# Six small moves in a two-layer gated cross-attention kernel: queues, PSUM rings and a halved last store

## The chip, the cores and the metric

The kernel runs on one core of a Trainium2 chip. A core has five engines with their own instruction queues: TensorE (PE, matrix products into PSUM), VectorE (DVE), ScalarE (ACT), GpSimd (POOL) and SyncE (SP, which here only starts transfers). ACT and POOL can start transfers too. Transfers run on 16 DMA engines beside them. The metric is the device time of one execution in microseconds (us).

## The reference

There are 16 sequences of 128 tokens with 512 features, and for each a context of 128 latents with 128 features. Two layers follow one another, each with an attention over the context and a feed-forward part, and each part is added to x through a gate:

```
x = x + tanh(g_xattn[0]) * L0_xattn(layernorm(x), ctx)   # 8 pairs of heads, low rank, rotary keys, softmax
x = x + tanh(g_ffn[0])   * L0_ffn(layernorm(x))          # 512 -> 2048 -> 512, LoRA experts, the best 2 of 8
x = x + tanh(g_xattn[1]) * L1_xattn(layernorm(x), ctx)   # 16 heads of 32, causal softmax
x = x + tanh(g_ffn[1])   * L1_ffn(layernorm(x))          # softmax-weighted sum of 8 products of rank 64
```

In layer 0 the query passes through three weights (Wq, w_kc_q and the rope weights W_qr) that don't depend on the tokens, so they can be multiplied together once. In layer 1 scores are q·k / sqrt(32) with later positions masked, and the feed-forward part is out = sum over k of alpha_k · U_k (V_k x), with alpha = softmax(relu(x W1 + b1) W2 + b2). Everything is float32.

## The kernel before

All matrix products have 128 rows of PSUM and 128 to 512 columns; four sequences (512 tokens) make a group g = 0 to 3. Sequences are loaded in the order 8 to 15, 0 to 7.

*Folding (L522 to L550).* The queries' three weights are folded into one, fq, pair of heads by pair of heads (p = 0 to 7): m_ps multiplies the rope weights wqr by wcq (L522), mT and mtr turn the product, f_ps (L546) multiplies it by wq. SP brings wcq, wqr and wq; ACT's queue brings the first wqr, the cosines and sines, the first four token tiles (256 KB each, L510), wkr and the gates. Between the folds, TensorE computes the keys k_ps0 and queries q_ps0 of the first group. VectorE takes the statistics of the first four token tiles as they land (L145, L146), ACT the root (L148), VectorE normalises (L158).

*Layer 0, attention.* The eight pairs of sequences are walked through with an order written out by hand. At the same time TensorE computes o_ps, the products of the output weight; VectorE and ACT copy them and VectorE and GpSimd form their sums (L632 to L640). `turn(v)` (L457) transposes two normalised token tiles on TensorE; only for v = 2 does it stand between the o_ps. Scores go through maximum (L685), exponential (ACT L696), reciprocal (L701), normalisation on GpSimd (L703), transposition within 32x32 blocks on VectorE (L709) and 16 sends by SP that move the blocks into eT.

*Layer 0, feed-forward.* For each group, `up_pair` computes the products hs_ps and ht_ps of a pair of hidden blocks in a form with fewer products, `spread` computes t_ps, the first low-rank products of all experts, and masks them by the chosen experts (L372), `adapt_pair` adds them (l_ps), and `down` multiplies back to 512 features. For groups 1 to 3 `spread` runs in the tail of the group before; for group 0 it follows the first `up_pair`.

*Layer 1.* A loop s = 2 to 17 has, in each step, `values` and `project` of sequence s − 2 (o_ps, y_ps), `score` of sequence s (v_ps and the scores s_ps, followed by L1316, L189, ACT L194, L199, GpSimd L201 and the transposition L1322 into eb), and `carry(s)`: ten 64 KB sends from eb to eT. Between these, a list `fill` of other units is taken by a table `plan`: queries (q_ps), and for the feed-forward part `hidden` (h_ps), `share_parts`, `ranks` (vx_ps) and `mixture` (my_ps). At s = 2, 6 and 10 `latents` transposes the latents of the next group (kv1tr_1 to kv1tr_3), and kv1tr_0 comes ahead of the loop. `tokens(g)` turns a group's normalised tokens by 16 sends, `ffn_tokens(g)` the same for the feed-forward part (xf).

*What sets the order.* TensorE and SP run in program order where `ordered` is set; VectorE's, ACT's and GpSimd's order is made by a scheduler from the dependences. An engine executes its queue in order, so one waiting instruction holds up all behind it. PSUM has three rings of 128x512 tiles: `ps_mm` with 4, `ps_tr` with 2 and `ps_acc` with 2 buffers; a tile can be written only when the reader of the tile that held its buffer before is done. In layer 1 q_ps, v_ps, h_ps, kv1tr and odd my_ps are in `ps_tr`, o_ps, y_ps and even my_ps in `ps_acc`. `evacuate` (L85, L87) copies PSUM by turns on VectorE and ACT; `drain` (L1204) copies on VectorE while a flag `near` is set and goes through `evacuate` otherwise. Transfers of SP and ACT share eight semaphores in turn, so each waits until the one eight before it has landed; those of GpSimd have eight of their own. `send` (L179) is a transfer on SP; `shared_send` (L1242) puts every third on GpSimd's queue and the others on SP.

Of the kernel before, what the change touches and what calls it, by code (L numbers as in the profile page):

```python
# [11 lines left out]
ALU = mybir.AluOpType  # L12
# [4 lines left out]
NB = 16  # L17
D = 512
ND = D // P
GB = 4  # L20
NG = NB // GB
# [21 lines left out]
def kernel(  # L43
# [9 lines left out]
    nc = tc.nc  # L53
# [9 lines left out]
    def mm_tile(name):  # L63
        return ps_mm.tile([P, 512], F32, tag="mm", name=name)

    def tr_tile(name):
        return ps_tr.tile([P, 512], F32, tag="tr", name=name)
# [7 lines left out]
    def pin(ins):  # L75
        if pinned[0]:
            tc.keep_in_program_order(ins)
# [33 lines left out]
    xs, xt = [None] * NB, [None] * NB  # L111

    def place(n):
        return (n + KEPT) % NB
# [11 lines left out]
    gate_f = [gates[:, 2 + i : 3 + i] for i in range(2)]  # L126
# [41 lines left out]
    def matmul(*args, **kw):  # L168
        ins = nc.tensor.matmul(*args, **kw)  # L169
        if ordered[0]:  # L170
            tc.keep_in_program_order(ins)

    def transpose(*args):
        ins = nc.tensor.transpose(*args)
        if ordered[0]:
            tc.keep_in_program_order(ins)
# [29 lines left out]
    half = GT // 2  # L206
# [154 lines left out]
    def spread(q):  # L361

        g = q.g
        t_ps = tr_tile(f"t_ps{g}")
        for c in range(ND):
            matmul(
                t_ps, a1_sb[:, c, :], q.xnT[:, c, :], start=(c == 0), stop=(c == ND - 1)
            )
        q.t1 = []
        for k in range(2):  # L370
            t = fh.tile([P, GT], F32, tag=f"t1_{k}", name=f"t1_{g}_{k}")
            nc.vector.scalar_tensor_tensor(  # L372
                t, t_ps, LORA_SCALE, q.selT[k], ALU.mult, ALU.mult
            )
            q.t1.append(t)


    with tc.tile_pool(name="a0", bufs=2) as ap, tc.tile_pool(name="a0s", bufs=3) as sp:
# [72 lines left out]
        def turn(v, which=(0, 1)):  # L451
            g, h = divmod(v, 2)
            if h == 0 and which[0] == 0:
                turned[g] = lnp.tile([P, ND, GT], F32, tag="xnT", name=f"xnT_a0_{g}", bufs=1)
            for i in which:
                xn = xns[v][i]
                tr = tr_tile(f"xtr_a0_{v}_{i}")  # L457
                for c in range(ND):
                    transpose(tr[:, ts(c, P)], xn[:, ts(c, P)], ident)
                dst = turned[g][:, :, ts(2 * h + i, P)]  # L460
                if v == 2:
                    pin(nc.vector.tensor_copy(dst, tr.rearrange("p (c t) -> p c t", t=P)))
                else:
                    evacuate(dst, tr.rearrange("p (c t) -> p c t", t=P))
# [5 lines left out]
        for kept, tag in ((k_r, "ca"), (q_r, "cb")):  # L470
            t = ap.tile([P, NPAIR, 2 * P], F32, tag=tag, name=f"{tag}_kq", bufs=1)
# [3 lines left out]
        with tc.tile_pool(name="fold", bufs=3, side="right") as fp:  # L475
# [31 lines left out]
            nc.scalar.dma_start(out=cos_sb, in_=cos_t)  # L507
            nc.scalar.dma_start(out=sin_sb, in_=sin_t)
            for n in range(GB):
                nc.scalar.dma_start(out=xs[n], in_=x[place(n)])  # L510
            nc.scalar.dma_start(out=wkr_sb, in_=wkr)
            nc.scalar.dma_start(out=gates[:, 0:2], in_=g_x.partition_broadcast(P))
            nc.scalar.dma_start(out=gates[:, 2:4], in_=g_f.partition_broadcast(P))
# [47 lines left out]
            for p in range(NPAIR):  # L561
# [13 lines left out]
                else:  # L575
                    tr = tr_tile("kvtr_0")
# [324 lines left out]
        for u in range(1, last + 1):  # L901
# [3 lines left out]
            v = u - 1  # L905
# [108 lines left out]
    for n in range(KEPT):  # L1014
        b = place(n)
# [48 lines left out]
    def up_pair(q, m):  # L1064

        g = q.g
        w = ups.pop((g, m))
        far = m + NF // 2
        bias, bias_f = bias1_sb[:, m : m + 1], bias1_sb[:, far : far + 1]


        ps = [tr_tile(f"hs_ps{g}_{m}_{n}") for n in range(2)]
        ps += [mm_tile(f"ht_ps{g}_{m}_{n}") for n in range(2)]

        def product(bank, cols, n):
            dst = ps[bank][:, cols]
            for c in range(2):
                matmul(dst, w[:, n, c, :], q.rhs[n][:, c, :], start=c == 0, stop=c == 1)
            return dst

        def part(name):
            return fh.tile([P, half], F32, tag=name, name=f"{name}_{g}_{m}", bufs=2)

        def biased_sum(dst, product, bias, other):
            nc.vector.scalar_tensor_tensor(dst, product, bias, other, ALU.add, ALU.add)

        base = tp.tile([P, GT], F32, tag="t", name=f"base_{g}_{m}")
        base_f = tp.tile([P, GT], F32, tag="t", name=f"base_{g}_{far}")
        p1, u2, u3, u4 = part("p1"), part("u2"), part("u3"), part("u4")
        nc.scalar.copy(p1, product(0, lo, 0))  # L1090
        biased_sum(base[:, lo], product(1, lo, 1), bias, p1)
        nc.vector.tensor_tensor(u2, product(2, lo, 4), p1, ALU.add)
        nc.vector.tensor_tensor(u3, product(0, hi, 5), u2, ALU.add)
        p5 = product(1, hi, 3)
        nc.vector.tensor_tensor(u4, p5, u2, ALU.add)
        biased_sum(base_f[:, hi], p5, bias_f, u3)
        biased_sum(base[:, hi], product(2, hi, 6), bias, u4)
        biased_sum(base_f[:, lo], product(3, lo, 2), bias_f, u3)
        if m + 2 < NF // 2:
            load_up(g, m + 2)  # L1100
        elif g + 1 < NG:
            load_up(g + 1, m + 2 - NF // 2)
        return base, base_f
# [98 lines left out]
    def drain(dst, src):  # L1202
        if near[0]:
            nc.vector.tensor_copy(dst, src)  # L1204
        else:
            evacuate(dst, src)
# [7 lines left out]
    kv, kvT, xa, ks, qs = {}, {}, {}, {}, {}  # L1214
# [3 lines left out]
        send(kv[g], kvc[g * GB : (g + 1) * GB].rearrange("b l d -> l b d"))  # L1218

    def latents(g):  # L1220
        tr = tr_tile(f"kv1tr_{g}")
        for i in range(GB):
            transpose(tr[:, ts(i, P)], kv[g][:, i, :], ident)
        kvT[g] = le.tile([P, GT], F32, tag="kvT", name=f"kv1T_{g}")
        drain(kvT[g], tr)
        if g + 1 < NG:
            load_latents(g + 1)

# [17 lines left out]
    def turn_all(dst, src, share=False):  # L1246

        for n, (t, k) in enumerate((t, k) for t in range(NK) for k in range(NK)):
            ends = dst[ts(k, BK), :, ts(t, BK)], src[ts(t, BK), :, ts(k, BK)]
            shared_send(n if share else 0, *ends)  # L1250
# [21 lines left out]
    def tokens(g, xb):  # L1272

        if g == 2:
            xa[g] = ap.tile([P, ND, GT], F32, tag="xf", name="xnT_a1_2", bufs=1)
        else:
            xa[g] = lnp.tile([P, ND, GT], F32, tag="xnT", name=f"xnT_a1_{g}", bufs=1)
        turn_all(xa[g].rearrange("p c (i t) -> p (c i) t", i=GB), xb)

    def queries(g, c):  # L1280
        q_ps = tr_tile(f"q1_ps{g}_{c}")
# [78 lines left out]
    xf, hs, al, avT, lTs = {}, {}, {}, {}, {}  # L1360
# [96 lines left out]
    def mixture(b):  # L1457
# [7 lines left out]
        residual(b, y_ps, gate_f[1])  # L1465
        done.append(b)

    done = []

    def store(keep):  # L1470
        while len(done) > keep:
            b = done.pop(0)
            send(out[b], xt[b])
# [34 lines left out]
    q = first  # L1508
    for g in range(NG):
        last = g == NG - 1  # L1510
        held = None
        for m in range(NF // 2):
            bases = up_pair(q, m)
            if g == 0 and m == 0:
                spread(q)
            if held is not None:
                adapt(q, m - 1, held)
            held = adapt_pair(q, m, bases)
            if g > 0 and m == 3:
                for b in range((g - 1) * GB, g * GB):  # L1520
                    moments1(b)
        if last:
            deviations1(slice(0, g * GB))
            aqo_sb = wp.tile([P, 2 * ND, D], F32, tag="w16", name="aqo_sb")
            for n, w in enumerate((a_wqT, a_woT)):
                send(aqo_sb[:, n * ND : (n + 1) * ND, :], w.rearrange("(c p) d -> p c d", p=P))
            xb = fh.tile([P, H, P], F32, tag="T", name="xb_a1_0")
            standard(xb, 0, mv1, rstd1, "a1", q.mixed)
            tokens(0, xb)
        else:  # L1530
            nxt = measure(g + 1)
            blocks(nxt, fh.tile([P, ND, GB, P], F32, tag="T", name=f"xb_f0_{g + 1}"),
                   q.mixed)
            turn_blocks(nxt)
        down(q, 0)
        adapt(q, NF // 2 - 1, held)
        bias_out(q)
        second_ranks(q)
        if last:
            break  # L1540
        for n in range(1, 7):
            down(q, n, {
                2: lambda: route_parts(nxt), 6: lambda: spread(nxt),
            }.get(n))
            if n == 2:
                route(nxt)
                quarter_tokens(nxt)
            elif n == 3:
                send_chosen(nxt)
        q = nxt  # L1550
# [11 lines left out]
    xb = le.tile([P, H, P], F32, tag="eT", name="xb_a1_1", bufs=1)  # L1562
# [23 lines left out]
    mw_sb = ap.tile([P, 3 * ND, D], F32, name="mw_sb", bufs=1)  # L1586
# [5 lines left out]
    for s in range(AHEAD, NB + AHEAD):  # L1592
        b = s - AHEAD
# [37 lines left out]
        if s in (3, 5, 7):  # L1631
            n = s // 2 - 1
# [6 lines left out]
    g = NG - 1  # L1639
# [8 lines left out]
    store(1)  # L1648
    for unit in units(ranks, g):
        unit()  # L1650
    for b in range(g * GB - 1, NB):
        mixture(b)
        store(1)
    store(0)

# [68 lines left out]
```

## Time and profile before

| quantity | value |
|---|---|
| time of three runs | 1509.08, 1509.17 (median), 1509.71 us |
| the profiled execution | 1511.77 us, span 1510.0 us, mean granted clock 0.998 |
| busy: TensorE | 1481.4 us, 98% of the span |
| busy: VectorE, ScalarE, GpSimd | 838.7 (56%), 436.6 (29%), 474.7 us (31%) |
| moved | 163.50 MB |

The profile is of one execution; the span runs from its first to its last instruction. "Waits" lists for each kind of instruction of an engine what ended the idle time before it: total, number, longest. "Timeline" lists instructions in order of time with start and duration, equal neighbours drawn together; in brackets is the idle time of the engine ahead of it and what ended it. The table by stage gives, for each stretch, its length, the busy time of the five engine columns (TensorE, its weight loads, VectorE, ScalarE, GpSimd) with counts, the granted TensorE clock, the DMA engines' busy share and GB/s. For a transfer the trace also has the moment at which it landed. A number behind a tile's name (o9, xn_0, eT(10)) says which sequence, group or pair it belongs to.

### The profile page before, as it was taken

To read this page: it belongs to the slowest core of one execution; us is meant where nothing else is said; L and a number is where in the kernel's file an instruction comes from. 1 tells how busy PE (TensorE), PEld (TensorE's weight loads), DVE (VectorE), ACT (ScalarE), POOL (GpSimd) and SP (SyncE) were. 2 spreads that over 40 slices of the span, in tenths; PEclk is the share of its full clock that TensorE was granted. 3 is DMA by queue.
4 is the path that set the end of the run, shared out by engine and by line. 5 is a ranking of instruction groups with operands and counts; after the bars stand their busy time and mean duration, and the time that the engine had idled before them with its cause. 6 is when DMAs were issued, how large, how long until landed. Compare 5 with 4: busy or idle time off the path is not lost. (4 is left out here: it accounts for less than half of the span.)

```text
span 1510.0 us, 19474 instructions
## 1 busy us (share of the span) xinstructions
PE 1481.4 (98%) x6744; PEld 996.9 (66%) x6744; DVE 838.7 (56%) x1723; ACT 436.6 (29%) x1430; POOL 474.7 (31%) x495
## 2 busy tenths in 40 slices
PE   8999999999999999999999999999999989999998
PEld 5667778878877666876678667866667444444444
DVE  3275654554566555655574656465756766747422
ACT  2252433443331222012211221022123555445310
POOL 2052633632522244113420433133313333424200
PEclk9999999999999999999999999999999999999999
DMA  9335567444446611642245224522253463535312
GB/s 318 105 77 92 146 178 178 96 113 100 91 77 161 232 63 70 157 138 73 74 112 158 74 74 105 144 94 73 74 137 72 69 113 71 89 54 85 69 28 98
DMA packets 360130, 163.50 MB, mean 108 GB/s; under 512 B 286528, under 2 KB 334400, under 8 KB 357856
## 3 DMA queue, kind: packets, MB, share of 16 engines
q1 hardware_dynamic: 356608, 156.54, 41.8%
q0 software_dynamic: 1856, 3.80, 1.8%
q10 hardware_dynamic: 1568, 1.90, 0.4%
q8 instruction: 54, 0.88, 0.3%
q14 instruction: 44, 0.36, 0.1%
HBM read 106.35 MB, written 18.09 MB: 82 GB/s over the span
## 5 line engine op out<-in xcount | busy, mean ns | idle before, releaser
L1124 POOL TENSOR_TENSOR near<-base,a 128x512 f32<-128x512 f32 x32 | 41.9, 1311 | 347.2 <-ACT base L1121 193.2
L703 POOL TENSOR_TENSOR e<-e,rden_a 128x512 f32<-128x512 f32 x64 | 66.1, 1040 | 181.8 <-DVE rden_a L701 181.8
L169 PE MATMUL l_ps<-t,b_sb 128*128 128x512 f32 x256 | 115.2, 592 | 1.4 <-DVE t L372 1.4
L169 PE MATMUL q_ps<-xnT_a,fq 128*128 128x256 f32 (+1 forms) x448 | 115.8, 410 | 0.0
L1121 ACT ACTIVATE a<-a 128x512 f32<-128x512 f32 x64 | 40.3, 629 | 257.3 <-DVE a L1120 257.3
L696 ACT ACTIVATE e<-s_ps,nmx_a 128x128 f32<-128x128 f32 x256 | 90.2, 384 | 80.9 <-DVE nmx_a L685 41.1
L201 POOL TENSOR_TENSOR e<-e,rden_a 128x512 f32<-128x512 f32 x64 | 66.4, 1039 | 149.6 <-DVE rden_a L199 147.4
L194 ACT ACTIVATE e<-e,nmx_a 128x128 f32<-128x128 f32 x256 | 98.8, 387 | 37.3 <-DVE nmx_a L189 37.3
L1120 DVE TENSOR_TENSOR a<-l_ps,base 128x512 f32<-128x512 f32 x64 | 44.0, 688 | 108.3 <-PE l_ps L169 108.3
L169 PEld LDWEIGHTS q_ps<-xnT_a,fq 128*128 128x128 f32 x448 | 84.8, 190 | 24.5 <-issue 12.5
L1186 DVE SCALAR_TENSOR_TENSOR x<-fy_ps,gw,x 128x256 f32<-128x256 f32 x112 | 46.5, 476 | 78.3 <-PE fy_ps L169 78.3
L169 PEld LDWEIGHTS l_ps<-t,b_sb 128*128 128x128 f32 x256 | 48.6, 190 | 61.7 <-issue 57.6
L169 PE MATMUL fy_ps<-ring,far 128*128 128x256 f32 x384 | 87.2, 380 | 0.0
L169 PE MATMUL y_ps<-fo_raw,c 128*128 128x256 f32 x384 | 85.8, 380 | 0.9 <-DVE c L85 0.9
L770 DVE SCALAR_TENSOR_TENSOR x<-y_ps,gates,x 128x256 f32<-128x256 f32 x112 | 48.7, 477 | 65.9 <-PE y_ps L169 65.8
L169 PEld LDWEIGHTS fy_ps<-ring,far 128*128 128x128 f32 x384 | 72.6, 190 | 13.6 <-issue 4.0
L169 PEld LDWEIGHTS y_ps<-fo_raw,c 128*128 128x128 f32 x384 | 72.3, 190 | 10.7 <-ACT c L87 1.0
L169 PE MATMUL ht_ps<-T,ring 128*128 128x256 f32 x256 | 65.7, 379 | 0.0
L169 PE MATMUL t_ps<-a,a_sb 128*128 128x512 f32 x128 | 65.4, 592 | 0.0
L169 PE MATMUL t_ps<-base,a_sb 128*128 128x512 f32 x128 | 65.4, 592 | 0.0
L169 PE MATMUL q_ps<-xnT_a,aqo_sb 128*128 128x512 f32 x128 | 59.8, 614 | 2.6 <-DMA xnT_a<-late 1.9
L169 PE MATMUL y_ps<-fo_sums,c 128*128 128x256 f32 x256 | 60.8, 385 | 1.5 <-DVE c L85 0.8
(256 smaller groups left out, 2957.2 us busy)
## 6 DMA issues: line engine op xcount, KB each, us to landing
ring<-w SPq DMA_DIRECT2D x32, 896.0 KB, 4.5
eT<-eb SPq DMA_DIRECT2D x312, 64.0 KB, 2.3
ring<-w SPq DMA_DIRECT2D x16, 1024.0 KB, 5.7
ring<-in_f_w SPq DMA_DIRECT2D x12, 1024.0 KB, 6.4
wq<-in_wq SPq DMA_DIRECT2D x8, 512.0 KB, 4.9
quarters<-in_f_w SPq DMA_DIRECT2D x32, 128.0 KB, 2.9
w<-sums SPq DMA_DIRECT2D x8, 512.0 KB, 3.6
quarters<-in_f_w SPq DMA_DIRECT2D x16, 256.0 KB, 3.3
```

What stands on the lines that cost most here:

```text
L169: ins = nc.tensor.matmul(*args, **kw)
L194: nc.scalar.activation(dst[:, ts(i, P)], src[:, ts(i, P)], AF.Exp, bias=nmx[:, i : i + 1], accum_out=den[:, i : i + 1],)
L201: nc.gpsimd.tensor_tensor(d3, d3, rden.unsqueeze(2).to_broadcast([P, 4, P]), ALU.mult)
L696: nc.scalar.activation(e[:, ts(i, P)], s_ps[:, ts(i, P)], AF.Exp, bias=nmx[:, i : i + 1], accum_out=den[:, i : i + 1],)
L703: nc.gpsimd.tensor_tensor(e3, e3, rden.unsqueeze(2).to_broadcast([P, 4, P]), ALU.mult)
L770: pin(nc.vector.scalar_tensor_tensor(dst, y_ps, gate_x[0], dst, ALU.mult, ALU.add))
L1120: nc.vector.tensor_tensor(a, l_ps, base, ALU.add)
L1121: nc.scalar.activation(a, a, AF.Gelu_apprx_tanh)
L1124: nc.gpsimd.tensor_tensor(mix, base, second, ALU.add)
L1186: nc.vector.scalar_tensor_tensor(dst, y_ps[:, ts(i, half)], q.first[:, t : t + 1], dst, ALU.mult, ALU.add,)
```

## The change

Six places change.

1. `turn`: for v = 2 the transposed tile is taken from the accumulator ring, not from the transposing ring.
2. The first four token tiles are loaded by SP, behind the second rope weights, not by ACT's queue.
3. `latents`: kv1tr is taken from the accumulator ring, and copied by ACT always. As `evacuate` is called less often, some of the copies after it change engine.
4. `tokens(3)`, the last query tokens, shares its 16 sends: 11 on SP and 5 on GpSimd.
5. The first `spread` stands before the first `up_pair`.
6. The last mixture, b = 15, is computed in two halves of 256 columns, one in each small ring, each with its own gated addition and its own store, on SP's and on ACT's queue.

```diff
-                tr = tr_tile(f"xtr_a0_{v}_{i}")
+                tr = (acc_tile if v == 2 else tr_tile)(f"xtr_a0_{v}_{i}")
...
             for n in range(GB):
-                nc.scalar.dma_start(out=xs[n], in_=x[place(n)])
+                nc.sync.dma_start(out=xs[n], in_=x[place(n)])
...
     def latents(g):
-        tr = tr_tile(f"kv1tr_{g}")
+        tr = acc_tile(f"kv1tr_{g}")
...
-        drain(kvT[g], tr)
+        nc.scalar.copy(kvT[g], tr)
...
-        turn_all(xa[g].rearrange("p c (i t) -> p (c i) t", i=GB), xb)
+        turn_all(xa[g].rearrange("p c (i t) -> p (c i) t", i=GB), xb, g == NG - 1)
...
+    def last_mixture(b):
+
+        g, i = divmod(b, GB)
+        for h, begin in enumerate((nc.sync, nc.scalar)):
+            half = slice(h * D // 2, (h + 1) * D // 2)
+            y_ps = (acc_tile, tr_tile)[h](f"my_ps{b}_{h}")[:, : D // 2]
+            for c in range(ND):
+                matmul(
+                    y_ps, avT[g][:, c, i], mw_sb[:, 2 * ND + c, half],
+                    start=(c == 0), stop=(c == ND - 1),
+                )
+            dst = xt[b][:, half]
+            nc.vector.scalar_tensor_tensor(
+                dst, y_ps, gate_f[1], dst, ALU.mult, ALU.add
+            )
+            begin.dma_start(out=out[b][:, half], in_=dst)
...
-            bases = up_pair(q, m)
             if g == 0 and m == 0:
                 spread(q)
+            bases = up_pair(q, m)
...
-    for b in range(g * GB - 1, NB):
+    for b in range(g * GB - 1, NB - 1):
         mixture(b)
         store(1)
     store(0)
+    last_mixture(NB - 1)
```

## The prediction, made before the changed kernel ran

> **What bounds the kernel now.** I read the head of the page first, then the chain of waits of TensorE, then the timeline and the table by stage around each long wait.
>
> ```profile
> span 1510.0 us, 19474 instructions
> PE 1481.4 (98%) x6744; PEld 996.9 (66%) x6744; DVE 838.7 (56%) x1723; ACT 436.6 (29%) x1430; POOL 474.7 (31%) x495
> ```
>
> TensorE is busy for 98% of the span. No matmul is removed, so only its idle time, some 24 us summed over all gaps, its clock and the tail can change. The waits of TensorE, in total, times, longest:
>
> ```profile
> PE m_ps L522 <- DMA wqr<-in_wqr: 6.5, 2, 4.0
> PE o_ps L169 <- DMA eT<-eb: 3.8, 1, 3.8
> PE v_ps L169 <- DVE x L184: 3.3, 1, 3.3
> PE q_ps L169 <- DMA xnT_a<-late: 1.9, 1, 1.9
> PE y_ps L169 <- DVE c L85: 1.7, 4, 0.9
> PE o_ps L169 <- PE xtr_a L174: 1.6, 2, 0.8
> PE l_ps L169 <- DVE t L372: 1.4, 1, 1.4
> PE kv1tr L174 <- DVE q L85: 0.9, 1, 0.9
> PE q_ps L169 <- ACT kv1T L87: 0.7, 1, 0.7
> ```
>
> The change touches nearly every row, so for each I ask what is late next. The step at 1312 to 1327 us decides most. Its timeline (start, duration, engine, operation) and its table by stage (the 0.50 is the granted clock, the last two columns DMA share and GB/s):
>
> ```profile
> 1312.23 0.18 DVE L199 RECIPROCAL rden_a<-den_a 128x4 f32<-128x4 f32 x1 [0.79 <-ACT e L194]
> 1312.73 0.71 DVE L1322 STREAM_TRANSPOSE eb<-e 128x512 f32<-128x512 f32 x1 [0.32 <-DMA late<-eb]
> 1314.32 0.72 DVE L184 SCALAR_TENSOR_TENSOR x<-y_ps,gates,x 128x512 f32<-128x512 f32 x1
> 1317.51 0.67 POOL L1242 DMA_DIRECT2D xf<-late  x1
> 1319.07 1.29 PE L169 MATMUL v_ps<-akv_sb,kv1T 128*128 128x512 f32 x2 [3.27 <-DVE x L184]
> 1322.31 4.18 PE L169 MATMUL my_ps<-mw_sb,late 128*128 128x512 f32 x8
> 1326.54 1.53 PE L169 MATMUL h_ps<-xf,mw_sb 128*128 128x512 f32 x3
> ...
> 1320.00:1322.00 2.00, 2.00 (x33) 1.71 (x32) 0.00 (x0) 0.59 (x1) 2.00 (x4) 0.50 0.87 96
> 1324.00:1326.00 2.00, 2.00 (x6) 0.76 (x4) 2.00 (x4) 1.61 (x9) 0.00 (x0) 1.00 1.03 138
> ```
>
> To be seen: VectorE's reciprocal stands ahead of a transpose that waits for a transfer; the last xf sends leave GpSimd at 1317.51 to 1320.42; the matmul that needs them, h_ps at 1326.54, starts the moment the last xf has landed (1326.24) and TensorE is free; and after the 3.27 us gap the clock is at half from 1319.90 to 1323.31.
>
> **The start.** The four first token loads (256 KB each) leave ACT's queue and follow the second rope weights on SP; x12 to x15 and the later weights shift behind them. Before, wqr_1 lands at 13.54 and x11 at 10.73; the bytes land along one curve (some 340 KB/us), so after the change wqr_1 lands near 11.0, TensorE's 2.44 us gap at 11.2 goes, and x11 lands near 13.5. What is late next: on VectorE the copies mT_1, xn_0 and kvT stand behind the statistics of x11. From 13.5, with the rows of before (statistics 0.69, aggregate 0.18, ACT table 1.28, root 0.30, reciprocal 0.17, normalise 0.55, kvT 0.69), k_ps0 starts near 17.7; it started at 17.89. Gain 0.2. Bounds: 2.45 if x11 isn't late, a loss of 0.7 if it lands 0.9 later than the curve says. I take 0.2, since the curve is this case's own.
>
> **The turns.** xtr_a0_2 goes into the accumulator ring. Before, o4 and o6 (both in the transposing ring) wait 0.81 each, for L638 of the folding two tiles back. In the other ring the tile that precedes has been copied by ACT (81.31 to 81.92) before the transposes at 82.82. I followed what each later tile waits for up to c_ps1 at 128.18, where eT_1 has 5.6 us to spare: no wait grows. Gain 1.6 (bounds 0.8, if one wait returns behind the other, to 1.6).
>
> **The spread.** Before, t_ps ends at 501.3 and l_ps waits for two L372 (0.69, 0.68): 1.38. After, t_ps runs at 491.85 to 495.3, and the second hs_ps needs its bank, so it waits for the same two L372. On VectorE these now stand behind statistics (493.9), ACT's root, reciprocal 0.17 and two normalisations of 0.55 (to 495.9), and end near 497.3; TensorE comes to the second hs_ps at 496.15. The new gap is 1.1 to 1.2, l_ps starts at 502.5 instead of 502.87. Gain 0.35 (bounds a loss of 0.3 and 1.4).
>
> **Latents 0 and 1.** In the accumulator ring kv1tr_0 doesn't wait for q (0.86); the query tile behind it then waits for part of that: gain 0.5. kv1T on ACT in place of the drain takes the 0.68 off the query after kv1tr_1: gain 0.7. The other copies change engine by turns (lT_0 to VectorE, k's swapped) with 1.4 us of slack where it is smallest. Together 1.2 (bounds 0 and 1.5).
>
> **Latents 3.** v_ps no longer shares a ring with my_ps1, so the 3.27 us wait goes. But o9 now follows y8 and kv1tr_3 in one ring and waits for y8's residual, and VectorE's order is another: one more transposition (0.67) stands before eb9, so the ten transfers of step 9 leave 0.6 later; the transpose eb10_0 at 1312.73, which waits for them, now stands before the reciprocal of 1312.23; y8's residual (0.72) before the next one. Step by step: eb10_0 at 1313.3, reciprocal 1313.95, GpSimd's L201 (1.04) to 1315.2, eb10_1 to 1316.0, residual to 1316.7 (so o9 at 1316.85, not 1314.72), L201 to 1317.8, and the fourth L201 ends near 1319.8, not 1317.57. Behind that L201 in GpSimd's queue stand five sends of xf and three of eT: 2.2 later. SP's seven eT sends wait for eb10_3 and move with them, so the jam that follows (DMA share 0.87 to 1.03) moves too: the last xf lands at 1328.4, h_ps starts at 1328.6. Loss 2.1. TensorE is done with my_ps2 at 1323.7 (it ended at 1326.49; 3.27 of gap and 1.7 of half clock go, 2.1 of o9's wait come). It then idles for 4.9 us; gaps of 3.84 and 3.27 here were each followed by 3.41 us at half clock, which cost 1.7 (eight q_ps took 5.40, elsewhere 3.70). Now that falls on h_ps, where nothing hides it. Loss 2.1 + 1.7 = 3.8 (bounds 0, if the sends catch up and the clock stays, and 5).
>
> **The last tokens.** Eleven of 16 sends stay on SP, five go to GpSimd, which is free from 1201.2 to the L201 of 1205.10. Before, 16 took 1204.25 to 1216.36 (0.757 each), and behind them stand mw_sb and seven sends of eT, the last landing at 1226.06; o4 starts at 1226.55. Five fewer would be 3.8. The nearest row is the same split for xf at 1388.23: 10.65 for its 11 and 5, so 12.11 − 10.65 = 1.45. The five sends also run beside the last three of step 3's carry (landings 0.6 apart when both queues send), so o3 at 1206.85 may start up to 2 later; o4's wait hides that. I take 1.8, near the row (bounds 1.45 and 3.8). The q wait of 1.9 goes, o4's stays.
> The Trainium skill, page DMA: Bandwidth & Descriptors, section Issuing engines are not separate DMA queues, says that transfers run on the same 16 engines whoever starts them, so that several starters save issue time alone. By it the gain ends where landings are the limit, an estimate of 16 × (0.757 − 0.6) = 2.5 and not 3.8; the xf row, 1.45, agrees.
>
> **The end.** The last residual is halved: 0.48 (the 128x256 row) after the last matmul instead of 0.75, and 128 KB instead of 256 KB to land after an issue of 0.33 (2.02 before). Gain 0.5 (bounds 0.2 and 0.8).
>
> **The sum.** 0.2 + 1.6 + 0.35 + 1.2 − 3.8 + 1.8 + 0.5 = 1.85 faster. It is made against the profiled execution, 1511.77 (span 1510.0, so 1.8 around it): 1509.9. The median of the three runs is 1509.17, 2.6 below that execution, so 1507.3 there. A measurement of this kernel can tell about 0.2% from no change, 3.0 us: this is no change.
>
> **The rivals.**
> First: the late xf costs nothing. If the sends catch up in the jam and TensorE waits less than the gaps that were followed by half clock, the 3.8 is 0: 5.65 faster, 1503.5. For it: SP's own eleven xf have landed by then, which thins the jam. Against it: the VectorE order above, which has no slack.
> Second: o4's wait shrinks until the clock holds. TensorE reaches o4 near 1222.3 with o3 late, the data at 1224.8: a gap of 2.5 with a further 1.7 saved. 1.85 + 1.7 = 3.55, 1505.6; with 3.8 from the sends 1503.6. For it: the 1.88 gap at 1217.16 had no drop behind it, and 2.5 lies nearer to that than to 3.27; against it: if o3 is on time the gap is 4.
> The Trainium skill, page TensorE: Matmul & The Clock Gate, section Why this matters for your kernels, asks for no idle gaps over about 3 us; by it the 2.5 us gap would keep full clock, and the trace's 3.27 and 3.84 agree.
> Third, slower: the lateness of step 10 passes on. eT(10) lands 2.2 later, the first transpose of step 11 waits for it, and if it repeats the shift for o11 and the transfers behind, each step costs 2.2 more and a half clock of 1.7. Two such steps, 7.8, give 1.85 − 7.8 = 5.95 slower, 1515.1; it is slower by over 0.2% once more than 4.85 is added. For it: the ring and the order are shared by all steps. Against it: before, that transpose starts at 1335.67, 7.9 after eT(10) has landed (1327.82).
>
> **How the numbers follow.** No change by the sum 0.43; first rival 0.24; second 0.17; third 0.16. The first two are the faster cases, 0.41 together; the third is slower, 0.16. The sum's own range is 1504.5 to 1510.5. The range takes in the faster cases with the better bounds of the sends, and half of the third: 1502.0 to 1512.5.
>
> **What would show it.** At the start no wait for wqr_1, but k_ps0 near 17.7. No o_ps wait for xtr_a. A wait of hs_ps for t of about 1.1. After 1310 no v_ps wait, an o_ps wait for the residual of y8, and an h_ps wait for xf of 4 to 5 us with half clock behind it. The last store 0.5 after what it was. I am wrong if h_ps waits less than 3 us for xf, or if new waits of TensorE appear in steps 11 to 13.

## The result and the profile after

| | before | after |
|---|---|---|
| median | 1510.2 us (22 runs, 1508.7 to 1513.4) | 1507.45 us (22 runs, 1504.9 to 1510.4) |
| ratio to before, 95% interval | | 0.9981 (0.9974 to 0.9987) |
| the profiled execution, its span | 1511.77 us, 1510.0 us | 1507.43 us, 1505.6 us |

The changed kernel is 2.75 us or 0.19% faster. The interval leaves out 1, so it is faster, but by less than the 0.2% that the prediction counted as a change; the forecast was 1507.3 and no change. Executions of one kernel differ by 2 to 3 us either way, so a step read from a single pair of profiles is a sample and not the mean: of the 4.4 us between the two spans, 1.6 is that the profiled execution of before lies 1.6 above its own median. Each kernel below was timed beside runs of before of its own (medians 1510.13, 1510.79 and 1510.98 for the three sets of experiments), so across sets the ratios are to be compared; differences of medians carry up to 0.8 us of this.

The head of the page after:

```profile
span 1505.6 us, 19498 instructions
PE 1480.5 (98%) x6752; PEld 1000.8 (66%) x6752; DVE 834.5 (55%) x1722; ACT 437.7 (29%) x1432; POOL 478.1 (32%) x500
```

TensorE is busy almost as long as before (1481.4), so the gain is idle time. Its chain of waits (total, times, longest):

```profile
PE m_ps L522 <- DMA wqr<-in_wqr: 4.3, 2, 4.0
PE h_ps L169 <- DMA eT<-eb: 3.0, 1, 3.0
PE o_ps L169 <- DMA xnT_a<-late: 2.3, 1, 2.3
PE o_ps L169 <- DMA eT<-eb: 2.2, 1, 2.2
PE o_ps L169 <- DVE x L184: 2.0, 1, 2.0
...
PE f_ps L546 <- DMA wq<-in_wq: 1.0, 1, 1.0
PE k_ps L169 <- DVE kvT L85: 0.9, 1, 0.9
PE kvtr L578 <- POOL kvr L404: 0.9, 1, 0.9
PE hs_ps L169 <- DVE t L372: 0.6, 1, 0.6
```

To be seen: the 3.3 of v_ps, the two 0.8 for xtr_a, the 0.9 of kv1tr, the 0.7 for kv1T and the 1.4 of l_ps are gone. In their place stand a wait of o9 for a residual (2.0), one of h_ps for the last xf (3.0), one of o3 for step 3's own transfers (2.3) and several of the start (f_ps, k_ps, kvtr). Two rows name a transfer that only landed about the same time: h_ps starts at 1321.31, 0.51 behind the last xf (1320.80), and o3, which reads its eT and not the tokens, starts at 1207.00, 0.45 behind the last of the ten sends that bring this eT (1206.55). In all nine kernels with the five sends on GpSimd o3 starts 0.45 to 0.48 behind that landing, which comes late as these five run beside the last of the ten.

I compared every instruction of TensorE with the same one of before and noted, stage by stage, by how much it had come earlier (+) or later (−). Eleven more kernels (below) gave the same table, so the last two columns are means over the thirteen profiles, with and without a part (before itself counts as 0; in the row of latents 3, with and without the changed order of VectorE):

| stage | predicted | after's profile | with the part, mean | without it, mean |
|---|---|---|---|---|
| start, to 83 us | +0.2 | −2.75 | −2.15 | +0.2 |
| turns | +1.6 | +2.1 | +2.1 | 0.0 |
| spread | +0.35 | +1.0 | +0.55 | +0.1 |
| latents 0 and 1 | +1.2 | +1.3 | +1.3 | 0.0 |
| last tokens, 1204 to 1233 us | +1.8 | +3.1 | +3.0 | +1.3 |
| the stretch of latents 3, 1310 to 1335 us | −3.8 | −1.8 | −2.8 | +0.3 |
| end | +0.5 | +0.8 | +0.7 | +0.1 |

A further 0.56 of after's profile lies at 844 us, where a product of hs_ps waits 0.29 in before and not in after. All six kernels with the first token loads on SP have this gain and none of the seven with them on ACT, so it belongs to that part; by what path was not followed. From 1335 us to the last part nothing moves (0.00).

### The profile page after: what moved, and what is told of

Its sections match the earlier page's. It is cut to its first block, busy times and chain, and to the rows that moved or that the text cites. A ratio compares the mean times of both kernels' runs of the same rounds, so it can differ in the third digit from the quotient of the medians.

```text
span 1505.6 us, 19498 instructions
## 1 busy us (share of the span) xinstructions
PE 1480.5 (98%) x6752; PEld 1000.8 (66%) x6752; DVE 834.5 (55%) x1722; ACT 437.7 (29%) x1432; POOL 478.1 (32%) x500
## 5 line engine op out<-in xcount | busy, mean ns | idle before, releaser
L169 PEld LDWEIGHTS fy_ps<-ring,far 128*128 128x128 f32 x384 | 72.8, 190 | 13.5 <-issue 4.0
L169 PEld LDWEIGHTS hs_ps<-xnT_f,ring 128*128 128x128 f32 x256 | 48.6, 190 | 19.8 <-issue 13.8
```

## The experiments

The theory behind the prediction: the stretch at 1310 costs because moving kv1tr_3 goes with another order of VectorE there; the start is neutral; the last tokens gain by shorter sending. The rivals: the cost is the wait that the new ring creates, and not the order, or the order comes from elsewhere than kv1tr_3; the start costs; the tokens' gain is the clock kept at o4.

### The start: first token loads back on ACT

The changed kernel, with one line undone.

```diff
-                nc.sync.dma_start(out=xs[n], in_=x[place(n)])
+                nc.scalar.dma_start(out=xs[n], in_=x[place(n)])
```

> The changed kernel with the first four token loads back on ACT's queue. Theory A (from the two traces): behind the second rope weights the tokens land at 12.6 to 14.5 instead of 7.5 to 10.7, the first keys start at 19.0 instead of 17.9, and the clock rises one window later; that cost TensorE 2.8 us by 21 us. Undone, TensorE stands at 83 us where it stood in the kernel before, the wait for wqr_1 of 2.4 is back, and the time is 2.8 shorter than the changed kernel's, about 0.996 of before. Theory B (the prediction's): the start is nearly neutral, 0.2 lost by undoing it, 0.998 of before.

Measured: 1506.73, ratio 0.9974 (0.9962 to 0.9985), 0.7 below the changed kernel, less than the interval can tell; theory A had 2.8, theory B 0.2 the other way, and the time decides between neither. Its profile has the 2.3 us wait of the second m_ps back, and yet its start is 2.2 earlier than after's. So the part that removes a wait for weights loses time. The timeline of TensorE, first of before:

```profile
13.67 1.55 PE L522 MATMUL m_ps<-wcq,wqr 128*64 128x128 f32 x12 [2.44 <-DMA wqr<-in_wqr]
...
17.89 1.87 PE L169 MATMUL k_ps<-kvT,wkr_sb 128*128 128x512 f32 x2
19.59 0.60 PE L164 MATMUL xtr_a<-ident,xn_a 128*128 128x128 f32 x4
20.03 0.83 PE L546 MATMUL f_ps<-m,wq 128*128 128x128 f32 x6
20.70 1.15 PE L164 MATMUL xtr_a<-ident,xn_a 128*128 128x128 f32 x8
```

and the same instructions of after:

```profile
12.08 1.55 PE L522 MATMUL m_ps<-wcq,wqr 128*64 128x128 f32 x12 [0.33 <-DMA wqr<-in_wqr]
...
19.02 2.08 PE L169 MATMUL k_ps<-kvT,wkr_sb 128*128 128x512 f32 x2 [0.94 <-DVE kvT L85]
20.89 1.06 PE L164 MATMUL xtr_a<-ident,xn_a 128*128 128x128 f32 x4
21.75 1.49 PE L546 MATMUL f_ps<-m,wq 128*128 128x128 f32 x6
23.03 1.58 PE L164 MATMUL xtr_a<-ident,xn_a 128*128 128x128 f32 x8
```

The wait is gone and m_ps starts 1.6 earlier, but k_ps0 starts 1.1 later, and then TensorE runs slow for longer: four xtr_a took 1.06 instead of 0.60, six f_ps 1.49 instead of 0.83 (the clock column reads 1.00 there in both, because the trace's record of the clock begins with its rise to full, at 19.42 in before and at 24.12 in after; the durations show the same). 1.1 later and some 1.6 of slow pace are the 2.75.

Why k_ps0 is late: by the landings of the transfers, the same bytes (all up to the second rope weights and the four token tiles) are in at 14.54 instead of 13.54. The view of the transfers in 0 to 20 us has a line of GB/s for each half microsecond, first before, then after:

```profile
GB/s 0 0 0 92 200 267 339 370 369 355 375 303 370 381 390 357 365 367 369 374 395 405 389 345 324 340 343 306 244 338 377 393 397 398 377 378 375 354 387 385
```

```profile
GB/s 1 0 0 55 230 313 392 357 328 242 300 332 244 366 376 313 385 310 330 355 385 390 385 336 315 306 331 303 320 297 331 357 311 225 344 402 395 390 382 381
```

From 4 to 7 us (the ninth to the fourteenth value) the mean is 302 instead of 359. The shared semaphores let a load start only when the one eight before it has landed, and with the tiles behind long weight loads on SP's queue the sends wait one for another. x9 goes out at 7.91, just behind wq_0 (landed at 7.86), x10 at 9.27 behind wkr (9.25), x11 at 10.30 behind kv (10.28). That the semaphores are the cause is read from these moments; no run here changes them alone.

### The last tokens: all sixteen sends back on SP

```diff
-        turn_all(xa[g].rearrange("p c (i t) -> p (c i) t", i=GB), xb, g == NG - 1)
+        turn_all(xa[g].rearrange("p c (i t) -> p (c i) t", i=GB), xb)
```

> The changed kernel with all 16 sends of the last query tokens on SP. Theory A: the split gives 1.5 of waits and 1.7 of clock. Undone, o3 no longer waits 2.3 for its transfers, q waits 1.9 again and o4 3.8, half clock follows o4, and the time is 3.2 longer than the changed kernel's, about 1.000 of before. Theory B: the clock after o4 was chance, as a gap of about 2 us is near the limit: only 1.5 longer, 0.999.

Measured: 1511.59, ratio 1.0003 (0.9993 to 1.0014). Without this part the whole gain of the change is gone: it is worth 0.0022 of the time, 3.3 us, as theory A had it. TensorE's waits of this kernel:

```profile
PE h_ps L169 <- DMA eT<-eb: 4.1, 1, 4.1
PE o_ps L169 <- DMA eT<-eb: 2.3, 1, 2.3
PE q_ps L169 <- DMA xnT_a<-late: 2.3, 1, 2.3
PE o_ps L169 <- DVE x L184: 2.0, 1, 2.0
```

The wait at o3 is gone, and q waits for the last tokens' transfers again. Theory A had o4 wait 3.8 with half clock behind it; here o4 waits 2.3 and keeps the clock, and the half clock falls behind the 2.3 of q. And h_ps, in a part that is the same as in after, waits 4.1 here and 3.0 there.

### Latents 3 in the old ring

The changed kernel with kv1tr_3 in the transposing ring and copied by `drain`.

```diff
-        tr = acc_tile(f"kv1tr_{g}")
+        tr = (tr_tile if g == NG - 1 else acc_tile)(f"kv1tr_{g}")
...
-        nc.scalar.copy(kvT[g], tr)
+        if g == NG - 1:
+            drain(kvT[g], tr)
+        else:
+            nc.scalar.copy(kvT[g], tr)
```

> The changed kernel with the last group's latents (kv1tr_3) in the transposing ring and drained as in the kernel before; groups 0 to 2 stay changed. Theory A (the two traces): this part alone lost 1.7, as a half clock window moved from under the xf transfers to behind h_ps. Undone, the o9 wait of 2.0 and the h_ps wait of 3.0 go, v_ps waits 3.3 again, and the time is 1.7 shorter than the changed kernel's, 0.997 of before. Theory B (the prediction's): 3.8 shorter, 0.9955.

Measured: 1507.33, ratio 0.9979 (0.9970 to 0.9989): no different from the changed kernel. Neither expectation held. The waits of o9 and h_ps are gone, but v_ps doesn't wait the 3.3 of before:

```profile
PE v_ps L169 <- DVE x L184: 6.0, 1, 6.0
```

and VectorE's order is still that of after, though the ring is that of before. The reciprocal that GpSimd waits for stands behind the transpose that waits for a transfer:

```profile
1307.90 0.71 DVE L1325 STREAM_TRANSPOSE eb<-e 128x512 f32<-128x512 f32 x1 [1.89 <-DMA late<-eb]
1308.54 0.14 DVE L199 RECIPROCAL rden_a<-den_a 128x4 f32<-128x4 f32 x1
1309.89 0.71 DVE L1325 STREAM_TRANSPOSE eb<-e 128x512 f32<-128x512 f32 x1 [1.22 <-POOL e L201]
```

So the order is not the ring's doing. With the first edit on top of this one:

```diff
-                nc.sync.dma_start(out=xs[n], in_=x[place(n)])
+                nc.scalar.dma_start(out=xs[n], in_=x[place(n)])
```

> The changed kernel with the tokens on ACT's queue and the last group's latents in the old ring. If the two losses are apart from one another, 2.8 and 1.7 add up: 4.5 shorter than the changed kernel's, about 0.995 of before. If they meet by way of the clock's windows, which stand at fixed times, less than the sum: 2 to 3 shorter.

Measured: 1506.59, ratio 0.9979 (0.9967 to 0.9990). Again v_ps waits long (5.4), and the stretch costs 2.8; the start is 3.1 earlier than in the run before, which has the tokens on SP, yet the median only 0.7. Neither expectation (4.5, or 2 to 3, below the changed kernel) held.

### What the order hangs on

`evacuate` copies by turns on VectorE and ACT. Each copy that `latents` gives to ACT directly takes one call out of that alternation. By the instruction lists, VectorE's order near 1310 is the changed one when an odd number of copies ahead of it have been taken out (three in the change: groups 0, 1 and 2), and that of before when it is an even number, whatever the ring. The counts seen are 0, 2 and 3; with one copy taken out no kernel was run. So I tried kernels with even counts. First, new ring and ACT copy for groups 0 and 1 alone:

```diff
-        tr = acc_tile(f"kv1tr_{g}")
+        tr = (acc_tile if g < 2 else tr_tile)(f"kv1tr_{g}")
...
-        nc.scalar.copy(kvT[g], tr)
+        if g < 2:
+            nc.scalar.copy(kvT[g], tr)
+        else:
+            drain(kvT[g], tr)
```

> The changed kernel with the new ring and ACT's copy for the latents of groups 0 and 1 alone; groups 2 and 3 as before. VectorE's instructions at 1296 to 1318 then stand in the order of the kernel before, since an even number of copies has left the alternation of evacuate. Theory A (order): the order, not the ring of kv1tr_3, made the reciprocals, GpSimd's L201 and the last xf sends some 2 later; with the old order v_ps waits 3.3 again as before, h_ps waits for nothing, the stretch 1300 to 1340 costs nothing against before, where it cost 1.8 in the changed kernel's trace and up to 4 in others: about 2 to 3 faster than the changed kernel, 0.9965 of before. Theory B (ring): as with the last group alone undone, v_ps waits 6, and the time stays at 0.998.

Measured: 1504.51, ratio 0.9960 (0.9947 to 0.9973), 2.9 below the changed kernel (3.2 by the ratios), as theory A had it. v_ps waits its 3.3 of before, h_ps nothing, and the stretch stands where it stood before (+0.2).

Second, the same with the token loads on ACT:

```diff
-                nc.sync.dma_start(out=xs[n], in_=x[place(n)])
+                nc.scalar.dma_start(out=xs[n], in_=x[place(n)])
```

> The same, and the first four token loads on ACT's queue again. The start's 2.4 and the stretch's 2 to 3 are gained on top of the changed kernel: 4.5 to 5 shorter, 0.995 of before, the fastest. If the order was not the cause, 0.997, as with the tokens' loads alone.

Measured: 1504.26, ratio 0.9962 (0.9948 to 0.9976): level with it, where 0.995 was expected: the start's 2.4 did not show in the time. The profiled execution, 1508.44, was its longest: a gap of 2.60 at o4 was followed by 6.8 us at half clock, which took back the 3 us that the tokens bring elsewhere.

Third, the whole change with all four groups in the new ring, and the alternation turned back by one step each time:

```diff
+        flip[0] ^= 1
         nc.scalar.copy(kvT[g], tr)
```

> The changed kernel, with the alternation of evacuate advanced by one at each of the latents' copies by ACT, so that all later copies alternate as if it had been called. All four groups stay in the new ring. VectorE's order at 1296 to 1318 is that of before. Theory A (order): o9 waits less than 0.5 instead of 2.0, the last xf leaves GpSimd 2 earlier than in the changed kernel; but as v_ps no longer waits, TensorE comes to h_ps early and waits there 4 to 5 for the xf that land where they landed before, and half clock follows: the stretch costs 1.7 against before, 0.9975. Theory B (ring): o9 waits 2.0 as in the changed kernel and nothing else moves, 0.998.

Measured: 1504.01, ratio 0.9957 (0.9946 to 0.9969). This is 3.4 us below the changed kernel (3.6 by the ratios), with one line more; only this version with the loads back on ACT (below) has a lower ratio. It is faster than either theory had it, as h_ps waits 2.0 and not 4 to 5. VectorE in this kernel, first, and in after:

```profile
1305.72 0.18 DVE L199 RECIPROCAL rden_a<-den_a 128x4 f32<-128x4 f32 x1 [0.79 <-ACT e L194]
1306.24 0.71 DVE L1323 STREAM_TRANSPOSE eb<-e 128x512 f32<-128x512 f32 x1 [0.34 <-DMA late<-eb]
1307.12 0.71 DVE L1323 STREAM_TRANSPOSE eb<-e 128x512 f32<-128x512 f32 x1 [0.16 <-POOL e L201]
...
1307.81 0.72 DVE L184 SCALAR_TENSOR_TENSOR x<-y_ps,gates,x 128x512 f32<-128x512 f32 x1
```

```profile
1308.01 0.71 DVE L1322 STREAM_TRANSPOSE eb<-e 128x512 f32<-128x512 f32 x1 [1.86 <-DMA late<-eb]
1308.65 0.14 DVE L199 RECIPROCAL rden_a<-den_a 128x4 f32<-128x4 f32 x1
1310.00 0.71 DVE L1322 STREAM_TRANSPOSE eb<-e 128x512 f32<-128x512 f32 x1 [1.22 <-POOL e L201]
1310.64 0.71 DVE L184 SCALAR_TENSOR_TENSOR x<-y_ps,gates,x 128x512 f32<-128x512 f32 x1
```

With the reciprocal ahead, GpSimd's normalisation overlaps the transpose's wait for its transfer; with it behind, VectorE waits 1.86 for the transfer and then 1.22 for GpSimd, and y8's residual, for which o9 waits, is pushed back. In this kernel o9 waits 0.6 and h_ps 2.0. The two causes now stand apart, by what the stretch of 1310 to 1335 us gains in each profile:

| | order of before | changed order |
|---|---|---|
| kv1tr_3 in the old ring | 0 (before), +0.2, +0.1, +1.1, +0.9, +0.3 | −2.7, −2.8 |
| kv1tr_3 in the new ring | +0.5, −0.5 | −1.8, −2.7, −4.2 |

By the means of the two columns the order costs about 3 us; the ring alone, with the order of before, shows no cost (+0.5 and −0.5 beside 0 to +1.1). Which of the shifted copies tips the scheduler was not followed further.

### The small parts, and each large part alone

Turns, spread and last halves alone on the kernel before:

```diff
-                tr = tr_tile(f"xtr_a0_{v}_{i}")
+                tr = (acc_tile if v == 2 else tr_tile)(f"xtr_a0_{v}_{i}")
...
-            bases = up_pair(q, m)
             if g == 0 and m == 0:
                 spread(q)
+            bases = up_pair(q, m)
...
-    for b in range(g * GB - 1, NB):
+    for b in range(g * GB - 1, NB - 1):
         mixture(b)
         store(1)
     store(0)
+    last_mixture(NB - 1)
```

> The kernel before with three parts alone: the turns in the other ring, the first spread moved, the last mixture in halves. From the two traces 2.1, 0.8 to 1.0 and 0.8: 3.7 to 3.9 shorter than before, 0.9975, with none of the start's loss and nothing moved in the last layer but the end. If the later waits take some of it back, 1 to 2.

Measured: 1506.84, ratio 0.9976 (0.9967 to 0.9986), 3.6 us faster. Turns are worth 2.1 in its profile (and 2.09 in every other that has them), the end 0.6, the spread 0.2.

The version with the order kept, and the token loads on ACT:

```diff
-                nc.sync.dma_start(out=xs[n], in_=x[place(n)])
+                nc.scalar.dma_start(out=xs[n], in_=x[place(n)])
...
+        flip[0] ^= 1
         nc.scalar.copy(kvT[g], tr)
```

> The kernel with VectorE's order kept, and the four first token loads back on ACT's queue. If the longer half clock at the start is a cost that reaches the end (0.5 to 0.7 in the comparison of the first experiment), this comes out 0.5 to 0.7 below the kernel with the order kept, near 1503.4, ratio near 0.9952. If the start's cost lies within what differs from run to run, it comes out level with it, 1504.0, ratio 0.9957, as with the pair that had latents 0 and 1 alone (1504.51 and 1504.26).

Measured: 1504.03, ratio 0.9952 (0.9939 to 0.9965): level with 1504.01 by the medians and 0.0005 (0.75 us) below by the ratios, which the intervals cannot tell apart, so neither expectation is decided. Its profiled start is 2.1 earlier, and its stretch 1.0 later, than that of the version with the loads on SP.

The token loads on SP as the only edit of the kernel before:

```diff
-                nc.scalar.dma_start(out=xs[n], in_=x[place(n)])
+                nc.sync.dma_start(out=xs[n], in_=x[place(n)])
```

> The kernel before with one edit: the four first token loads on SP behind the second rope weights. By the prediction's step it gains 0.2 (1510.0). By the ledger of the profiled runs it loses: wqr_1 lands earlier, but k_ps0 starts near 19.0 and the half clock lasts to 23.6, some 1.9 to 2.8 slower, 1512 to 1513. By the comparison of the kernels with and without it (0.3 to 0.7) it loses about 0.5, 1510.7. In the profile: wait for the second wqr below 2.5, k_ps0 behind 18.5, half clock beyond 22 in the second and third case.

Measured: 1512.46, ratio 1.0010 (1.0001 to 1.0019): slower by 1.5 us, with the interval from 0.15 to 2.9. Its profile loses 2.7 by 83 us, and k_ps waits 0.9 for kvT as in after. The part is a loss by itself. Where it was undone inside other versions the medians gave back 0.0, 0.25, 0.7 and 0.7, less than this and less than the 2.3 by which the profiles of the two groups differ at 83 us (1.75 with the 0.56 at 844); each of these differences is within the intervals, so the loss as a single edit is shown, and its size is known only to lie between 0.15 and 2.9.

The last tokens as the only edit of the kernel before:

```diff
-        turn_all(xa[g].rearrange("p c (i t) -> p (c i) t", i=GB), xb)
+        turn_all(xa[g].rearrange("p c (i t) -> p (c i) t", i=GB), xb, g == NG - 1)
```

> The kernel before with one edit: five of the sixteen sends of the last tokens on GpSimd. By the prediction's step it gains 1.8 with the q wait gone and o4's wait left at about 2, 1508.4. If o4's gap falls below what the clock drops behind, it gains 1.7 more: 3.5, 1506.7. If the delay of o3 (2.3) takes back what the queries gain, it is level with before, 1510.2. VectorE's order around 1310 stays that of before, so v_ps waits about 3.3 and h_ps under 1.

Measured: 1507.73, ratio 0.9979 (0.9970 to 0.9987): 3.2 us faster, with the interval from 2.0 to 4.5. That lies between the expected 1.8 and 3.5. In its timeline o3 waits (for its own eT, landed at 1208.62, and not for the transfer that the row names), and o4 no longer does:

```profile
1209.10 1.08 PE L169 MATMUL o_ps<-late,v 128*32 128x128 f32 x32 [2.64 <-DMA xnT_a<-late]
1210.11 1.71 PE L169 MATMUL v_ps<-akv_sb,kv1T 128*128 128x512 f32 x2
1211.75 2.09 PE L169 MATMUL s_ps<-k,late 32*128 32x128 f32 x32
...
1224.33 1.08 PE L169 MATMUL o_ps<-eT,v 128*32 128x128 f32 x32
```

After the 2.64 TensorE runs at half clock: the two v_ps take 1.71 (1.13 in after, at full clock), s_ps 2.09 (1.18). Nearly all of that is hidden: o4's data, eT(4), land at 1224.02, and TensorE, late as it is, is at o4 at 1224.33. Before, they landed at 1226.06 and o4 started at 1226.55. Less the 0.5 by which this execution was ahead already, o4 starts 1.75 sooner; and the half clock behind o4, 1.7 before, is gone. Together 3.45 in the profile, 3.2 by the timed runs.

## Why the prediction was right, point by point

The total was right, 1507.3 for 1507.45, and so was "no change", narrowly. That it was met to 0.15 us is luck. The forecast gain was 1.85 and the measured one 2.75 (2.0 to 3.9), and the median of three runs that it was taken from, 1509.17, lies 1.0 below that of all 22; the two errors cancel. Within the sum the loss of a wrong step was balanced by gains that came out larger, and one cause was misjudged.

- **The start was wrong.** The step said +0.2 with bounds from +2.45 to −0.7; it lost 1.5 as a single edit, and 2.3 at 83 us by the profiles, of which 0.56 comes back at 844. Its first half held: wqr_1 landed early (11.95, forecast 11.0) and the 2.44 gap shrank to 0.33. The error is in "the bytes land along one curve": the same bytes took 1.0 us longer, x11 landed at 14.54 instead of 13.5 and k_ps0 started at 19.02 instead of 17.7. And the step had no term for TensorE's slow pace behind it, which lasted longer.
- **The turns** gave 2.1 instead of 1.6: neither o4 nor o6 waits. The upper bound, 1.6, counted the waits only. Without a wait TensorE also begins the next product before the transposes have ended, 0.43 behind the first of them where it was 1.42, twice.
- **The spread** gave 0.46 by the difference of the means, forecast 0.35; hs_ps waits 0.59 and not 1.1.
- **Latents 0 and 1** gave 1.3 for 1.2.
- **Latents 3** is the step whose price held and whose cause was half right. The waits came as listed: no v_ps wait, o9 1.97 (forecast 2.1), then h_ps with half clock behind it, 3.04 in after and 4.1 in two other kernels (forecast 4 to 5; below 3 would have been the sign of being wrong). The cost was 2.9 (against groups 0 and 1 alone) to 3.4 (against the order kept), forecast 3.8. The step worked its loss out from VectorE's other order, and the runs show that this order does cost it. But the step took the order to come with kv1tr_3's own move; undoing that move alone left the order and the loss in place, and the order follows the number of copies taken out of `evacuate` ahead of it. The lateness of the transfers was mis-sized. In after the last xf send left GpSimd at 1317.13, which is 2.1 later than before once the lead of 5.35 is taken off (forecast 2.2), but the five sends landed in 2.3 to 3.8 us each instead of up to 5.98. So the last xf, at 1320.80, landed 0.1 earlier than before by the same reckoning, and the 1.8 lost there is the half clock alone; in the first two experiments h_ps starts 1.0 and 1.2 late. The sends did catch up, as the first rival had it, but with TensorE at h_ps 3 us sooner the clock still dropped, so the 3.8 did not become 0.
- **The last tokens** gave 3.2 (2.0 to 4.5) and not 1.8. The term of the sends was right: with this part alone o4 starts 1.75 sooner, in after 1.4. So was the lateness of o3, which o4's wait hides. What is missing is the clock. The step had o4's wait stay; it shrank from 3.83 to 2.15 in after, to 1.10 in the first experiment and to nothing with this part alone, and the half clock behind it, 1.7, went with it. That is the second rival's mechanism at the second rival's price (1.8 + 1.7 = 3.5). It is shown against the one profile of before alone: in the three other profiles without the part o4 waits 1.5 to 2.3 at full clock and the half clock falls behind q, and by the means of all profiles the part is worth 1.7. The runs say 3.2 and 3.3; how much of that is the clock stays open. The Trainium skill, page DMA: Bandwidth & Descriptors, section Issuing engines are not separate DMA queues, says that transfers run on the same 16 engines whoever starts them; the estimate of 2.5 made by it for the sends is a ceiling that the 1.4 to 1.75 of these profiles stay below, near the row of the xf sends, 1.45.
- **The end** gave 0.7 for 0.5.
- **The third rival**, slower by lateness handed on from step to step, did not come: from 1335 us to the last part every instruction of TensorE keeps its lead to within 0.01.

Added up by the timed runs: the three small parts 3.6, the start −1.5 and the tokens 3.2 are 5.3. The measured 2.75 leaves −2.55 for the latents, where 1.2 − 3.8 = −2.6 was forecast; the intervals of the terms are 1 to 1.5 us either way, so this close an agreement is more than the runs can show. Added up by the means of the profiles (the difference of the table's last columns) the sum is 0.8, and 1.4 with the 0.56 at 844. That this is 1.3 below the measurement is not explained (the tokens alone are 1.5 less than timed); single steps differ by up to 2 us between profiles of the same code, and four profiles or fewer stand behind some means.

## What to carry to other kernels

A helper that alternates engines couples places that have nothing to do with one another: after taking one call out of it, compare the instruction order of every engine further down, and restore the alternation where that order mattered. A load that leaves a queue also lets what was behind it go ahead, so follow all transfers of the first microseconds, and not the one that was waited for. Before pricing a wait, ask what later wait would hide it: a delay of 2.6 us and a half clock at o3 cost next to nothing here, because o4's data came as late.

## What the runs showed that was not expected

The half clock does not follow from the length of a gap alone. Over all thirteen profiles I took TensorE's gaps of 1.1 us and more from 100 us on and the granted clock in the five microseconds behind each. None of 10 gaps of 1.10 to 1.97 us was followed by half clock; all of 10 gaps of 3.04 us and more were; of the 20 between, 12 were and 8 were not, in no order of length: 2.01 and 2.03 were, 2.79 and 2.86 were not. Two such gaps in the table by stage, the 2.15 at 1220.7 of after, and the 2.01 at 1315.5 of the version with the order kept:

```profile
1222.00:1224.00 2.00, 1.11 (x33) 0.94 (x33) 2.00 (x5) 0.00 (x0) 0.00 (x0) 1.00 0.01 1
1224.00:1226.00 2.00, 2.00 (x5) 0.96 (x6) 2.00 (x5) 0.58 (x1) 0.00 (x0) 1.00 0.00 0
```

```profile
1318.00:1320.00 2.00, 2.00 (x5) 0.89 (x4) 0.35 (x3) 2.00 (x11) 1.54 (x2) 0.68 0.77 102
1320.00:1322.00 2.00, 2.00 (x3) 0.79 (x3) 0.18 (x1) 0.67 (x4) 1.50 (x2) 0.50 0.42 70
```

The clock column behind the first reads 1.00, behind the second 0.68 and 0.50.

What decides can be read from the moments at which the traces have the clock change. In every profile they lie on a grid of 3.41 us, which stands elsewhere in each execution. With TensorE's idle time added up within each stretch of that grid, all 22 drops from 100 us on come at the end of a stretch with 1.99 us or more of it, and no stretch at full clock with 1.98 or less is followed by one. So the 2.15, which the grid divides into 1.46 and 0.69, and even the 2.86 (1.80 and 1.06) kept the clock, and the 2.01, which lies within one stretch, lost it. The ends of matmuls are modelled in the trace, so the mark is about 2 us.

The Trainium skill, page TensorE: Matmul & The Clock Gate, section Why this matters for your kernels, asks for no idle gaps over about 3 us. The runs agree above 3.04, and show that 2 us is not safe either. At 1.7 us a time, the place of the grid alone moves a single execution by as much as most parts of this change are worth, so parts of this size are to be judged by many runs and not by one pair of profiles.
